# Two bf16 products of zeros per batch, into the unused columns of an attention kernel's PSUM tile

## The chip, the cores and the metric

The kernel runs on one core of a Trainium2 chip. The metric is the device time of one execution in microseconds. The kernel before takes 3329.91 us, the median of three runs (3328.71 to 3332.3).

## The reference, cut to what matters

Four layers of a graph network run one after the other on 6250 nodes with 128 features and 106,250 edges sorted by target (each node has a loop to itself); each layer ends in a residual and a layer norm. The change lies in the last, a graph attention with H = 3 heads:

```python
alpha = a_src[row2] + a_dst[col2] + a_edge
alpha = jnp.where(alpha >= 0, alpha, NEG_SLOPE * alpha)
m = jax.ops.segment_max(alpha, col2, num_segments=n)
ex = jnp.exp(alpha - m[col2])
denom = jax.ops.segment_sum(ex, col2, num_segments=n)
attn = ex / denom[col2]
msg = attn[:, :, None] * xp[row2]
agg = jax.ops.segment_sum(msg, col2, num_segments=n)
y = (agg.reshape(n, H * OUT) + gat_bias) @ lin_W + lin_b
```

Then comes the sum of `x` and `y`, a layer norm with weights, the outer residual and the last layer norm. The kernel sums the rows of `x` by attention weight first, and multiplies by the product of the two weight matrices (`mh`) afterwards, in `end`.

## The kernel before, in words

The function `by_windows` holds all four layers. The first three fill the first 2250 us of the profiled execution: sums over edges as bf16 products of one-hot matrices (L819), gathers by GpSimd (L774), and dense layers. They are not touched.

The attention works in NBT = 208 batches of BT = 4 tiles of 128 edges. The targets of a batch lie in a window of BW = 40 nodes, so H x BW = 120 columns hold the weights of a tile. A batch has S = 6 slices: the last tile of the batch before, its own four, and one with the loops of its nodes.

- `fetch(b)` (L1061) gathers the source rows of four tiles with four indirect DMAs from GpSimd's queue (L1065), into one of eight buffers `rows3`. It runs AHEAD = 5 batches ahead.
- `weigh(b)` loads the loop rows (SyncE, L1119), forms the logits `z` (L1121, `lrelu` L315), a mask (L1129, L1134), and `w`, the masked logits of 6 x 120 columns (L1136). Six TensorE transposes bring it to PSUM (`w_p`, L1141), and VectorE takes the maximum per head and node (`mx`, L1144).
- `power(b)` brings that maximum back to 128 partitions with a transpose into a slot of the PSUM tile `both` (L1148), subtracts it (VectorE, L1151), and ScalarE takes the exponential (L1153).
- `gather(b)` makes the weighted sums: six fp32 products accumulate in the PSUM tile `o`, 120 x 132 (L1162; each is two records in the trace). Columns 0 to 127 are features and 131 is the sum of weights. Then the reciprocal (VectorE, L1164), the scaling (ScalarE, L1166), a transpose into `both` (L1168), and the copy into `acc` (L1169).
- `end(blocks)` (products at L1102) finishes 500 nodes, after each sixteenth or so batch.

The source loop issues `power(b - 1)`, `gather(b - 2)`, `fetch(b + 5)`, `weigh(b)` and, where due, `end`. A scheduler then lays out the instructions of each engine anew; each engine works through its own list in order. So the order of L1141, L1148, L1162 and L1168 on TensorE is not that of the source, and changes from batch to batch. Every fourth batch the window bases are read into registers (L307).

Of the kernel before, what the change touches and what calls it, by code (L numbers as in the profile page):

```python
# [8 lines left out]
F32 = mybir.dt.float32  # L9
# [10 lines left out]
F = 128  # L20
# [5 lines left out]
H = 3  # L26
# [14 lines left out]
BT, NBT, BW = 4, 208, 40  # L41
# [5 lines left out]
BF16 = mybir.dt.bfloat16  # L47
# [8 lines left out]
def gnn_kernel(ctx: ExitStack, tc: tile.TileContext, a: dict, out: bass.AP):  # L56
# [135 lines left out]
    with tc.If(ordered) as cond:  # L192
        by_windows(tc, a, out, consts, ix)
# [9 lines left out]
def by_windows(ctx: ExitStack, tc: tile.TileContext, a: dict, out: bass.AP, consts, ix):  # L203


    nc = tc.nc
# [50 lines left out]
    def by_block(table, blocks):  # L257
        return table[blocks[0] * PB:(blocks[-1] + 1) * PB, :].rearrange("(b p) f -> p b f", p=PB)
# [5 lines left out]
    def row_over(x, nb):  # L264

        return x.rearrange("p (b f) -> p b f", b=1).to_broadcast([PB, nb, x.shape[1]])
# [33 lines left out]
    def bases(at, n, engine, last=N - 1):  # L300

        got = {}

        def of(g):
            if g % 4 == 0:
                m = min(4, n - g)
                _, v = nc.values_load_multi_w_load_instructions(  # L307
                    ix["base"][0:1, at + g:at + g + m], engines=[engine], min_val=0, max_val=last,
                    skip_runtime_bounds_check_because=WITHIN)
                got.update({g + i: y for i, y in enumerate(v)})  # L310
            return got[g]
        return of

    def lrelu(x):
        nc.vector.scalar_tensor_tensor(x, x, 0.2, x, op0=OP.mult, op1=OP.max)  # L315
# [120 lines left out]
    for c in range(GC):  # L436
        for k in range(RT):
            nc.tensor.matmul(counts[:, c:c + 1], lhsT=below[:, k, c * 128:(c + 1) * 128], rhs=oneb,
                             start=(k == 0), stop=(k == RT - 1))
# [270 lines left out]
    with tc.tile_pool(name="l0w", bufs=2) as work, \  # L710
# [5 lines left out]
        for blocks in CHUNKS:  # L716
# [18 lines left out]
            for j in range(nb):  # L735
                for m in range(4):
                    nc.tensor.matmul(yp[:PB, j, :], lhsT=ht[:, m, j * PB:(j + 1) * PB], rhs=w2[:, m, :],  # L737
                                     start=(m == 0), stop=(m == 3))
# [319 lines left out]
    S = BT + 2  # L1058
    rows = {}

    def fetch(b):  # L1061
        own = min(BT, 831 - b * BT)
        r = rows[b] = gp.tile([128, BT, XW], F32, name="rows3")
        for j in range(own):
            nc.gpsimd.indirect_dma_start(  # L1065
                out=r[:, j, :], out_offset=None, in_=x3,
                in_offset=bass.IndirectOffsetOnAxis(ap=ix["src"][:, BT * b + j:BT * b + j + 1], axis=0))
        if own < BT:
            nc.vector.memset(r[:, own:BT, :], 0.0)
# [11 lines left out]

    l3b = ctx.enter_context(tc.tile_pool(name="l3b", bufs=1))
    acc = l3b.tile([128, H, NW], F32, name="acc3")
    of_sp, of_dve = bases(NG, NBT, SP), bases(NG, NBT, DVE)
    with tc.tile_pool(name="lr", bufs=5) as lrp, \
            tc.tile_pool(name="zb", bufs=4) as zbp, tc.tile_pool(name="ob", bufs=2) as obp, \
            tc.tile_pool(name="wb", bufs=3) as wbp, tc.tile_pool(name="fin", bufs=1) as fin, \
            tc.tile_pool(name="fps", bufs=1, space=bass.MemoryType.PSUM) as fps, \
            tc.tile_pool(name="tps", bufs=2, space=bass.MemoryType.PSUM) as tps, \
            tc.tile_pool(name="ops", bufs=2, space=bass.MemoryType.PSUM) as ops, \  # L1090
            tc.tile_pool(name="mps", bufs=1, space=bass.MemoryType.PSUM) as mps:
        both = mps.tile([128, 4, H, BW], F32, name="both")
        loops_, zs, ws, ms = {}, {}, {}, {}

        def end(blocks):


            b0, nb = blocks[0], len(blocks)
            p = fps.tile([128, 4, F], F32, name="fp")
            for j, b in enumerate(blocks):  # L1100
                for h in range(H):
                    nc.tensor.matmul(p[:PB, j, :], lhsT=acc[:, h, b * PB:(b + 1) * PB], rhs=mh[:, h, :],  # L1102
                                     start=(h == 0), stop=(h == H - 1))
            x = xn[:PB, b0:b0 + nb, :]
            y, z, o = (fin.tile([128, 4, F], F32, name=n)[:PB, :nb, :] for n in ("yf", "zf", "of"))
            nc.vector.tensor_tensor(y, x, row_over(cb[:PB], nb), op=OP.add)
            nc.vector.tensor_add(y, y, p[:PB, :nb, :])
            layernorm(z, y)
            nc.vector.tensor_tensor(z, z, row_over(lng[:PB], nb), op=OP.mult)
            nc.vector.tensor_tensor(z, z, row_over(lnb[:PB], nb), op=OP.add)  # L1110
            nc.vector.tensor_add(z, z, x)
            layernorm(o, z)
            nc.sync.dma_start(by_block(out, blocks), o)

        def weigh(b):

            r = rows[b]
            loop = loops_[b] = lrp.tile([128, XW], F32, name="loop")
            nc.sync.dma_start(loop, x3[ds(of_sp(b), 128), :])  # L1119
            z = zs[b] = zbp.tile([128, S, H], F32, name="z")  # L1120
            nc.vector.tensor_add(z[:, 1:1 + BT, :], r[:, :, F:F + H], zed[:, BT * b:BT * (b + 1), :])  # L1121
            lrelu(z[:, 1:1 + BT, :].rearrange("p j h -> p (j h)"))
            nc.scalar.copy(z[:, S - 1, :], loop[:, F + H + 1:F + 2 * H + 1])
            if b:
                nc.scalar.copy(z[:, 0, :], zs.pop(b - 1)[:, BT, :])
            else:
                nc.vector.memset(z[:, 0, :], 0.0)
            oh = wbp.tile([128, S, 1, BW], F32, name="oh3")
            nc.vector.tensor_tensor(oh[:, :, 0, :],  # L1129
                                    iota[:, 0:BW].rearrange("p (j w) -> p j w", j=1).to_broadcast([128, S, BW]),  # L1130
                                    ix["relb"][:, b, :].rearrange("p (j w) -> p j w", w=1).to_broadcast([128, S, BW]),
                                    op=OP.is_equal)

            nc.vector.tensor_scalar(oh, oh, -1.0, -LOW, op0=OP.add, op1=OP.mult)  # L1134
            w = ws[b] = wbp.tile([128, S, H, BW], F32, name="w3")
            nc.vector.tensor_tensor(w, oh.to_broadcast([128, S, H, BW]),  # L1136
                                    z.rearrange("p j (h w) -> p j h w", w=1).to_broadcast([128, S, H, BW]),
                                    op=OP.add)
            tp = tps.tile([H * BW, 2, 512], F32, name="w_p")
            for j in range(S):  # L1140
                nc.tensor.transpose(tp[:, j // 3, j % 3 * 128:(j % 3 + 1) * 128],  # L1141
                                    w[:, j, :, :].rearrange("p h w -> p (h w)"), ident)
            mx = ms[b] = zbp.tile([H * BW, 1], F32, name="mx")
            nc.vector.tensor_reduce(mx, tp[:, :, 0:384], AX.XY, OP.max)  # L1144

        def power(b):
            mb = both[:, b % 2]
            nc.tensor.transpose(mb.rearrange("p h w -> p (h w)"), ms.pop(b).to_broadcast([H * BW, 128]),  # L1148
                                ident[:H * BW, :H * BW])
            wf = ws[b].rearrange("p j h w -> p j (h w)")  # L1150
            nc.vector.tensor_tensor(wf, wf, mb.rearrange("p (j h) w -> p j (h w)", j=1)  # L1151
                                    .to_broadcast([128, S, H * BW]), op=OP.subtract)
            nc.scalar.activation(wf, wf, AF.Exp)  # L1153

        def gather(b):
            wf = ws.pop(b).rearrange("p j h w -> p j (h w)")
            loop = loops_.pop(b)
            r0 = rows.pop(b - 1)[:, BT - 1, 0:F + H + 1] if b else loop[:, 0:F + H + 1]
            o = ops.tile([H * BW, F + H + 1], F32, name="o")
            for j in range(S):  # L1160
                rr = r0 if j == 0 else loop[:, 0:F + H + 1] if j == S - 1 else rows[b][:, j - 1, 0:F + H + 1]
                nc.tensor.matmul(o, lhsT=wf[:, j, :], rhs=rr, start=(j == 0), stop=(j == S - 1))  # L1162
            rd = zbp.tile([H * BW, 1], F32, name="rd")
            nc.vector.reciprocal(rd, o[:, F + H:F + H + 1])  # L1164
            on = obp.tile([H * BW, F], F32, name="on")
            nc.scalar.activation(on, o[:, 0:F], AF.Copy, scale=rd)  # L1166
            ot = both[:, 2 + b % 2]
            nc.tensor.transpose(ot.rearrange("p h w -> p (h w)"), on, ident[:H * BW, :H * BW])  # L1168
            nc.vector.tensor_copy(acc[:, :, ds(of_dve(b), BW)], ot)  # L1169


        for b in range(NBT + 2):
            if 1 <= b <= NBT:
                power(b - 1)
            if b >= 2:
                gather(b - 2)
            if b + AHEAD < NBT:
                fetch(b + AHEAD)
            if b < NBT:
                weigh(b)  # L1180
            for k, d in enumerate(DONE):
                if d == b - 2:
                    end(CHUNKS[k])
# [692 lines left out]
```

## Time and profile before

| | |
|---|---|
| median of 3 runs | 3329.91 us (3328.71 to 3332.3) |
| the profiled execution | 3577.21 us |
| its span, first to last instruction | 3575.3 us |
| mean granted TensorE clock over the span | 0.82 |
| before 2250 us / after it | 0.87 / 0.74 |
| TensorE busy, span | 2624.6 us (73%) |
| VectorE busy, span | 1837.7 us (51%) |
| GpSimd busy, span | 1671.1 us (47%) |
| ScalarE busy, span | 910.8 us (25%) |
| busy after 2250 us (1325.3 us): PE / DVE / POOL / ACT | 800.3 / 845.6 / 806.5 / 361.2 us |

Times are of one profiled execution, which is longer than the runs without a profile. PE is TensorE's products, PEld its weight loads, DVE VectorE, ACT ScalarE, POOL GpSimd, SP SyncE. A row of slices cuts the span in 40 parts and shows the busy tenths of each; PEclk is the granted share of TensorE's clock in tenths. "x <- y" in the list of waits reads: x's engine sat idle until y had ended. "issue", "remote" and "an unknown queue" are waits of which the trace does not show the end. The ends of TensorE's products are modelled.

### The profile page before, as it was taken

What the parts mean: (1) busy time and instruction counts of PE and PEld (TensorE: products, weight loads), DVE (VectorE), ACT (ScalarE), POOL (GpSimd) and SP (SyncE); (2) the same over time, 40 slices, a digit from 0 to 9 for tenths busy, and PEclk for the clock granted to TensorE, in tenths of its full rate; (3) what the DMA queues carried; (4) which work ended last, traced back from release to release, by engine and by line L of the source; (5) the groups of instructions that cost most, each with busy time, mean ns of one, the idle gap of its engine ahead of it and who ended that gap; (6) DMA issues with size and microseconds to landing.
All of it is one profiled execution on the core that took longest, in us unless ns stands there. A gap on an engine that the chain in (4) does not pass through costs nothing.

```text
span 3575.3 us, 43560 instructions
## 1 busy us (share of the span) xinstructions
PE 2624.6 (73%) x14544; PEld 1618.5 (45%) x14544; DVE 1837.7 (51%) x6113; ACT 910.8 (25%) x1657; POOL 1671.1 (47%) x1684
## 2 busy tenths in 40 slices
PE   2788879899995599999787893666565666666565
PEld 1334335544442344445343342555554555555554
DVE  4899994478214800000211122666565666666666
ACT  0587874300002400002100010222222222222222
POOL 3000002277607755430556424666666666666662
PEclk9677779999997599999898896777777777777777
DMA  5588871387751356563665553222222222222221
GB/s 155 167 278 279 274 248 48 105 245 228 220 164 51 82 181 205 182 183 96 184 179 153 169 166 90 52 58 58 54 61 58 56 57 58 55 60 59 57 58 33
DMA packets 333524, 461.85 MB, mean 129 GB/s; under 512 B 43998, under 2 KB 217854, under 8 KB 332933
## 3 DMA queue, kind: packets, MB, share of 16 engines
q1 hardware_dynamic: 250754, 278.98, 26.2%
q0 software_dynamic: 54912, 105.86, 12.4%
q10 hardware_dynamic: 27624, 74.14, 5.6%
q8 instruction: 117, 1.92, 0.2%
q14 instruction: 117, 0.96, 0.1%
HBM read 375.30 MB, written 83.36 MB: 128 GB/s over the span
## 4 chain that ended last, share of the span: by engine, by line
PE 52%; DVE 22%; issue 12%; DMA 4%; POOL 3%; another core or an unknown queue 3%; ACT 2%; DVEq 1%; SPq 0%; ACTq 0%; POOLq 0%
PE sums L819 25%; PE o L1162 10%; DVE okey L616 5%; DVE olow L614 4%; PE w_p L1141 4%; POOL nd L416 2%; DVE w L1151 2%; PE both L323 2%; DVE w L1136 1%; PE yp L995 1%; ACT w L1153 1%; PE yp L737 1%; PE fp L1102 1%; DVE mx L1144 1%
## 5 line engine op out<-in xcount | busy, mean ns | idle before, releaser
L1065 POOL DMA_INDIRECT rows<-x,srca x831 | 841.5, 1013 | 490.3 <-issue 213.4
L819 PE MATMUL sums<-piece,arena 125*128 125x500 bf16 x4500 | 1021.1, 383 | 51.1 <-issue 40.0
L819 PEld LDWEIGHTS <-arena 125*128 125x128 bf16 x4500 | 435.6, 98 | 591.4 <-issue 122.4
L774 POOL DMA_INDIRECT row<-table,srca x549 | 542.1, 987 | 335.7 <-issue 142.5
L1162 PE MATMUL o<-rows,w 128*120 128x132 f32 x2078 | 440.1, 364 | 245.1 <-issue 132.2
L1162 PEld LDWEIGHTS o<-rows,w 128*120 128x120 f32 x2078 | 378.1, 255 | 290.1 <-issue 159.7
L619 ACT CAST arena<-made 128x1000 bf16<-128x1000 f32 (+1 forms) x260 | 313.5, 1262 | 63.9 <-PE made L617 55.9
L1153 ACT ACTIVATE w<-w 128x720 f32<-128x720 f32 x208 | 167.0, 803 | 521.6 <-DVE w L1151 368.5
L617 PE MATMUL made<-okey,olow 128*128 128x250 bf16 x1000 | 248.4, 330 | 62.4 <-ACT arena L619 28.4
L616 DVE TENSOR_SCALAR okey<-iok,key 128x250 bf16<-128x250 bf16 x1000 | 289.6, 290 | 0.0
L1141 PE MATMUL w_p<-ident,w 128*120 128x128 f32 x1248 | 230.7, 328 | 65.1 <-DVE w L1136 39.1
L1144 DVE TENSOR_REDUCE mx<-w_p 120x1 f32<-120x768 f32 x208 | 198.0, 952 | 151.7 <-PE o L1162 82.6
L1151 DVE TENSOR_TENSOR w<-w,both 128x720 f32<-128x720 f32 x208 | 187.1, 900 | 162.0 <-remote 89.1
L614 DVE TENSOR_SCALAR olow<-iob,low 128x128 bf16<-128x128 bf16 x1000 | 254.7, 255 | 0.0
L1141 PEld LDWEIGHTS w_p<-ident,w 128*120 128x120 f32 x1248 | 187.2, 169 | 80.3 <-issue 49.6
L325 ACT COPY by_node<-both 128x128 f32<-128x128 f32 (+1 forms) x48 | 12.7, 265 | 756.6 <-PE both L323 479.8
L334 DVE TENSOR_TENSOR onehot<-iota,relg 128x384 f32<-128x384 f32 x118 | 64.2, 547 | 272.7 <-PE both L323 140.9
L617 PEld LDWEIGHTS <-olow 128*128 128x128 bf16 x1000 | 108.0, 113 | 184.9 <-DVE okey L616 89.6
L1136 DVE TENSOR_TENSOR w<-oh,z 128x720 f32<-128x720 f32 x208 | 186.7, 898 | 0.2 <-DVE acc L1169 0.2
L690 POOL MEMSET ea<- 128x128 f32 x1 | 0.5, 465 | 397.9 <-PE sums L323 397.9
L1168 PE MATMUL both<-ident,on 120*128 120x120 f32 x208 | 70.3, 338 | 108.2 <-DVE w L1151 95.2
L1148 PE MATMUL both<-ident,mx 120*128 120x120 f32 x208 | 73.0, 351 | 91.2 <-DVE acc L1169 69.6
(283 smaller groups left out, 3188.5 us busy)
## 6 DMA issues: line engine op xcount, KB each, us to landing
piece<-edges SPq DMA_DIRECT2D x300, 625.0 KB
edges<-arena ACTq DMA_DIRECT2D x100, 625.0 KB
ea<-in_edge_attr_dram SPq DMA_DIRECT2D x69, 768.0 KB
loop<-x SPq DMA_DIRECT2D x208, 68.0 KB
rows<-x,srca POOLq DMA_INDIRECT x831
row<-table,srca POOLq DMA_INDIRECT x549
eat<-in_edge_attr_dram POOLq DMA_DIRECT2D x28, 236.0 KB
table<-xn SPq DMA_DIRECT2D x24, 250.0 KB
```

The source lines that it names most:

```text
L614: nc.vector.tensor_scalar(o, iob, low[:, g:g + 1], None, op0=OP.is_equal)
L616: nc.vector.tensor_scalar(w, iok, key[:, g:g + 1], None, op0=OP.is_equal)
L617: nc.tensor.matmul(p[:, i, 0:NB5 * GD], lhsT=o, rhs=w, start=True, stop=True)
L619: nc.scalar.copy(to, p[:, 0:n, 0:NB5 * GD].rearrange("p i (h d) -> p i h d", d=GD))
L774: nc.gpsimd.indirect_dma_start(out=r[:, j, :], out_offset=None, in_=table, in_offset=bass.IndirectOffsetOnAxis(ap=ix["src"][:, t:t + 1], a ...
L819: nc.tensor.matmul(p, lhsT=xp[:PB, h, i, :], rhs=t[:PB, :, (h - h0) * SC:(h - h0 + 1) * SC], start=(h == 0 and i == 0), stop=(h == NB5 - 1 ...
L1065: nc.gpsimd.indirect_dma_start(out=r[:, j, :], out_offset=None, in_=x3, in_offset=bass.IndirectOffsetOnAxis(ap=ix["src"][:, BT * b + j:BT ...
L1136: nc.vector.tensor_tensor(w, oh.to_broadcast([128, S, H, BW]), z.rearrange("p j (h w) -> p j h w", w=1).to_broadcast([128, S, H, BW]), op= ...
L1141: nc.tensor.transpose(tp[:, j // 3, j % 3 * 128:(j % 3 + 1) * 128], w[:, j, :, :].rearrange("p h w -> p (h w)"), ident)
L1144: nc.vector.tensor_reduce(mx, tp[:, :, 0:384], AX.XY, OP.max)
L1151: nc.vector.tensor_tensor(wf, wf, mb.rearrange("p (j h) w -> p j (h w)", j=1) .to_broadcast([128, S, H * BW]), op=OP.subtract)
L1162: nc.tensor.matmul(o, lhsT=wf[:, j, :], rhs=rr, start=(j == 0), stop=(j == S - 1))
```

## The change

A tile `zeros` of 128 x 512 bf16 is filled with zeros once by GpSimd. The PSUM tile `o` grows from 132 to 512 columns[...]. In each batch a product of zeros (120 x 380, bf16) is written into its columns 132 to 511 before the six products of sums, and another after them. Nobody reads those columns.

```diff
+    zeros = l3b.tile([128, 512], BF16, name="zeros")
+    nc.gpsimd.memset(zeros, 0.0)
...
+        def idle(to):
+
+            nc.tensor.matmul(to, lhsT=zeros[:, 0:H * BW], rhs=zeros[:, 0:to.shape[1]], start=True, stop=True)
+
...
-            o = ops.tile([H * BW, F + H + 1], F32, name="o")
+            o = ops.tile([H * BW, 512], F32, name="o")
+            idle(o[:, F + H + 1:])
             for j in range(S):
                 rr = r0 if j == 0 else loop[:, 0:F + H + 1] if j == S - 1 else rows[b][:, j - 1, 0:F + H + 1]
-                nc.tensor.matmul(o, lhsT=wf[:, j, :], rhs=rr, start=(j == 0), stop=(j == S - 1))
+                nc.tensor.matmul(o[:, 0:F + H + 1], lhsT=wf[:, j, :], rhs=rr, start=(j == 0), stop=(j == S - 1))
+            idle(o[:, F + H + 1:])
```

The scheduler sees the new instructions, and its order of the others changes too, on TensorE, VectorE and ScalarE from the first batches of the attention on. SyncE's order stays, and GpSimd's but for the one memset.

## The prediction

> **What bounds the kernel now.** First the page: the time slices say where the change acts. It touches only the attention loop, so I looked for the first product into `o` (L1162), at 2251.8 us of a span of 3575.3 us. Everything before it is issued in the same order in both builds.
>
> ```profile
> PE   2788879899995599999787893666565666666565
> DVE  4899994478214800000211122666565666666666
> POOL 3000002277607755430556424666666666666662
> PEclk9677779999997599999898896777777777777777
> ```
>
> From slice 26 on no engine is full: PE, DVE and POOL are busy six tenths each, and PE was granted 0.7 of its clock, against 0.9 in the stage of L819. The loop has 208 batches in some 1308 us, 6.3 us each. Next came the chain of work that ended last, restricted to 2250 to 3560 us, and the waits there.
>
> ```profile
> by line: PE o L1162 26.7%; issue 20.5%; PE w_p L1141 10.3%; another core or an unknown queue 7.9%; DVE w L1151 4.2%; DVE w L1136 3.9%; ACT w L1153 3.4%; DVE mx L1144 3.0%; PE fp L1102 2.9%; PE both L1148 2.7%; PE both L1168 1.5%; DVEq L307
> ```
>
> (the waits: who, for what, us in total, times, longest)
>
> ```profile
> POOL rows L1065 <- PE o L1162: 176.2, 81, 11.4
> ...
> PE o L1162 <- ACT w L1153: 110.1, 80, 6.7
> ...
> DVE w L1151 <- remote: 89.1, 29, 6.4
> ```
>
> PE's products are 44% of this chain (26.7+10.3+2.9+2.7+1.5), so what PE's clock does counts. The gathers wait for PE (their row buffers are freed by L1162), not PE for them. PE in turn waits for the exponential. The stage is a ring of PE, DVE and ACT, and no single engine is the limit.
>
> Then the granted clock, in stretches cut on its own steps, 3.41 us long (columns: stretch, length, busy PE, PEld, DVE, ACT, POOL with counts, clock, DMA):
>
> ```profile
> 2614.42:2617.83 3.41, 1.71 (x9) 1.67 (x9) 3.02 (x8) 0.43 (x2) 2.80 (x3) 0.50 0.22 47
> 2617.83:2621.25 3.42, 3.31 (x16) 2.90 (x15) 2.36 (x5) 1.21 (x4) 2.53 (x3) 0.50 0.29 62
> 2621.25:2624.66 3.41, 2.46 (x21) 2.22 (x21) 3.23 (x8) 1.25 (x3) 2.77 (x3) 1.00 0.34 82
> 2624.66:2628.07 3.41, 1.04 (x10) 0.80 (x8) 1.05 (x2) 0.00 (x0) 2.50 (x4) 1.00 0.18 41
> 2628.07:2631.49 3.42, 2.39 (x11) 2.39 (x11) 0.22 (x2) 1.25 (x3) 1.51 (x2) 0.50 0.36 82
> ```
>
> The 0.7 is a mean of two values, 0.50 and 1.00. A stretch with PE busy 3.31 of 3.42 us is followed by a fast one; a fast stretch with 1.04 of 3.41 is followed by a slow one. I did this for all 360 stretches from 2331 us on. Of 77 changes to fast, 73 came after a busy share of 0.85 or more. Of 76 changes to slow, 68 came after a share under 0.45. The fast share is 48%. What it is worth shows in two rounds of the same order, slow then fast:
>
> ```profile
> 2618.45 1.23 PE L1162 MATMUL o<-rows,w 128*120 128x132 f32 x4
> 2619.68 1.53 PE L1162 MATMUL o<-rows,w 128*120 128x132 f32 x6
> 2623.22 0.71 PE L1162 MATMUL o<-rows,w 128*120 128x132 f32 x4 [0.95 <-ACT w L1153]
> 2623.88 0.84 PE L1162 MATMUL o<-rows,w 128*120 128x132 f32 x6
> ```
>
> Starts of neighbouring records are 0.22 us apart when slow, 0.11 when fast. With 12 records for `o`, 6 for `w_p` and one for each of the two into `both`, PE needs 20 x 0.22 = 4.4 us a batch slow, 2.2 us fast.
>
> **The change part by part.** *The products themselves.* The nearest row is the bf16 product of L819: 1021.1 us for 4500 products of 500 columns, 0.227 us each at clock 0.9 to 1. For 380 columns that is 0.173 us fast and, doubled, 0.345 us slow. Two in each of 208 batches: 72 us of PE time if always fast, 144 us if always slow. Their weight loads lie beside products, as L819's do. How much is on the path? The built order puts the first one ahead of `o`'s first matmul, which waits for the exponential (the 110.1 us above), mostly in a gap; the second comes right after the last `o`. Behind that second one are queued the six transposes L1141, for which the maximum L1144 waits. The reciprocal L1164 now also waits for it: in the built program its semaphore value counts the second product, and in 28 of 208 batches also a transpose L1148 that stands between. L1164 comes after the 0.9 us subtraction L1151 on DVE, which hides most of that. If all were on the path it would cost 208 x 2 x (0.67 x 0.173 + 0.33 x 0.345) = 96 us at the fast share I expect below; by PE's 44% of the chain 42 us; I take 30 us, a third, since one of the two stands before a wait. It can't gain by itself.
>
> *The clock.* Each product adds 0.05 (fast) to 0.10 (slow) to the busy share of a stretch. 27 of the 76 falls to slow came from shares of 0.35 to 0.45: I count those as saved, so falls go from 76 of 172 fast stretches (0.44) to 49 (0.28). Of 110 slow stretches that stayed slow 30 had shares of 0.70 to 0.85: those I count as raised, so rises go from 77 of 187 slow stretches (0.41) to 107 (0.57). Balance: 0.57/(0.57+0.28) = 0.67 fast, up 0.19. Over the PE timeline the 73 rounds of the commonest order lasted 6.09 us when over three quarters slow (23 rounds) and 5.03 us when over three quarters fast (27), 1.06 us less. 0.19 x 208 x 1.06 = 42 us gained. The PE time alone (2.2 x 0.19 x 208 x 44%) would give 38. Bounds: 0, and 0.19 x 208 x 2.2 = 87 us.
>
> Here the Trainium skill ("TensorE: Matmul & The Clock Gate", Part 1) speaks differently: the clock falls only after an idle window of about 3.4 us. By that two products a batch, which leave no stretch idle, would end every fall, and 0.52 x 208 x 1.06 = 115 us would come back. The trace refuses it: falls come from stretches busy up to 0.45. I go by the rows. The same page (Part 4) says that transposes do not count as PE activity in the same way, which would leave the shares lower; but a threshold over all products misplaces 12 of 358 stretches, one without transposes 49. They count here.
>
> *The order.* The scheduler lays the loop out anew. In 91 of the 207 rounds of before, a transpose L1148 stands inside or ahead of L1141's six in a cycle of three rounds; by the PE timeline these 91 took 573 us, 6.30 each, the commonest order 5.85. In the new build these cycles are gone (163 rounds are of the common kind). 91 x 0.45 = 41 us. But 29 of these 91 hold the 29 unexplained waits of L1151 (89.1 us); if those are not due to the order nothing is left. Bounds 0 and 41; I take 20.
>
> *The rest.* One memset on POOL, 0.5 us (the nearest is L690's, 0.465 us), queued among the first gathers, which are five batches ahead: nothing. Without that lead 0.5 us. SyncE's order is the same; POOL's gathers follow in the same order. The new tile fills a bank, with as many buffers as before: no new wait for `o` beyond its readers, which the transpose L1168 has waited for already.
>
> Sum: 30 - 42 - 20 = -32 us, from 3577.2 us (span 3575.3) to about 3545. The profiled execution is 247 us longer than the median of 3329.9; the stage's chain holds 28% of "issue" and unknown waits, some of which may exist only under the profiler. I carry the difference over as it is: 3298 us.
>
> **The rivals.** *Slower: the price without the clock.* In the stretches just after the last `o`, the second product delays L1141, the maximum, and so the next subtraction, in every batch; if the fast share does not rise, the two cost 2 x (0.48 x 0.173 + 0.52 x 0.345) = 0.53 us a batch, 109 us of PE time. A third of that is 36 us, with no gain: 3366 us. It decides from a rise of the fast share under 30/(208 x 1.06) = 0.14. For it: 41 of the 76 falls came from shares under 0.35 or so, and two products do not mend these. Against it: the thresholds are sharp, and zeros keep PE busy as any data does.
>
> *No change: POOL sets the pace.* While a gather does not wait it starts 1.25 us after the one before (0.94 busy, 0.30 "issue"), so 831 need 1039 us of the stage's 1308. If the 247 us that the profile adds lie in this stage, 1061 are left without it, and the gathers are nearly the bound: whatever PE gains is hidden, 3330 less a few us. Against it: POOL waited 176 us for PE.
>
> *The full gain.* Falls nearly end, as the skill's rule has it, and the order gives 20 as above: 30 - 115 - 20 = -105, 3225 us. For it speaks that each fall saved leaves PE faster and the ring shorter; against it the 41 falls from low shares.
>
> **How the numbers follow.** Mine (3265 to 3321, about 3298): 0.40. The full gain: 0.12. POOL's pace, within 0.2%: 0.15. Slower: 0.33. 0.2% (7 us) is about what a measurement of this kernel can tell from no change. Faster is 0.40+0.12 = 0.52. The range, 3240 to 3372, leaves out about 0.08 below (part of the full gain) and 0.12 above (products wholly on the path in slow stretches). Alone, my case has 3265 to 3321.
>
> **What would show it.** The mean clock after 2250 us: 0.74 before, (1+0.67)/2 = 0.84 by my count; under 0.80 the slower rival decides. The new products' starts 0.17 us ahead of what follows. L1141's and L1164's waits on PE: longer by under 0.15 us a batch. The unexplained waits of L1151: gone if they were the order's. POOL's waits for L1162: from 176 us towards 0 if POOL becomes the bound. I am wrong if the clock rises and the time doesn't, or if the fast share stays where it is.

## The result and the profile after

The kernel after takes 3321.15 us, the median of 8 runs (3315.76 to 3323.84), beside 3333.56 us for the kernel before on the same chip (8 runs, 3328.71 to 3342.4). The ratio is 0.9958, with an interval of 0.9947 to 0.9969. That makes it 14 us faster (12 us between the two medians, since the ratios here are not plain quotients of medians), where 32 had been forecast. The profiled execution of after took 3318.93 us, and its span is 3317.1 us.

The slices of the span of after:

```profile
PE   2788788979999549999988899366666666666666
DVE  4899996448722380000031112287767777777766
POOL 2100002058751776553056652467777777777774
PEclk6676778989999759999999899688888888888878
```

In the attention (slice 26 on) the granted clock is 8 where the page of before had 7, as forecast. But VectorE and GpSimd are busier too, 7 where they had 6, although they do the same work: the stage itself is shorter, 1142 us from the first product into `o` to the end (2174.7 to 3317.1), against 1324 (2251.8 to 3575.3). Those 181 us are far more than the runs differ. So the two pages can't be laid side by side as "before and after"; something else lies between them.

The chain of work that ended last, and the waits, from 2250 to 3317 us:

```profile
by line: DMA rows<-x,srca 17.6%; PE o L1169 16.7%; issue 10.9%; DVE w L1157 10.1%; POOL rows L1065 7.8%; ACT w L1159 6.9%; DVE w L1142 4.9%; DVE mx L1150 3.2%; PE w_p L1147 2.7%; PE fp L1104 2.6%; DVE acc L1177 1.5%; PE both L1154 1.5%; DVE
```

```profile
PE o L1169 <- ACT w L1159: 239.4, 167, 13.0
DVE z L1127 <- DMA rows<-x,srca: 196.1, 82, 4.5
...
POOL rows L1065 <- PE o L1169: 46.0, 63, 3.3
```

A row stands here that the chain of before did not have: the arrival of gathered rows, 17.6%, and with the gathers themselves (L1065) a quarter of the chain. The first logits of a batch wait 196.1 us for rows. In the page of before they never waited for them, and the gathers waited 176.2 us for PE. The waits of L1151 on "remote", 89.1 us, are gone.

The new products in the groups of the page of after, and one pair in the timeline (columns there: start, length, instruction):

```profile
L1119 PE MATMUL o<-zeros 128*120 128x380 bf16 x416 | 133.1, 352 | 0.7 <-POOL zeros L1085 0.7
```

```profile
2178.86 0.33 PE L1119 MATMUL o<-zeros 128*120 128x380 bf16 x1
2179.03 0.82 PE L1147 MATMUL w_p<-ident,w 128*120 128x128 f32 x6
```

A record lasts 0.33 us, but what follows starts 0.17 us after it. Over all pairs without a gap the median is 0.16 us at the full clock and 0.32 us at half: the forecast of 0.173 and 0.345 us a product was right.

### The profile page after: what moved, and what is told of

Read it like the earlier page. It is cut to its first block, busy times and chain, and to the rows that moved or that the text cites. A ratio compares the mean times of both kernels' runs of the same rounds, so it can differ in the third digit from the quotient of the medians.

```text
span 3317.1 us, 44206 instructions
## 1 busy us (share of the span) xinstructions
PE 2536.9 (76%) x14960; PEld 1547.6 (47%) x14960; DVE 1831.8 (55%) x6113; ACT 902.3 (27%) x1657; POOL 1675.9 (51%) x1685
## 4 chain that ended last, share of the span: by engine, by line
PE 35%; DVE 13%; DMA 10%; POOL 7%; issue 7%; ACT 3%; DVEq 1%; POOLq 0%; SPq 0%; ACTq 0%
PE sums L819 21%; DMA rows<-x,srca 6%; PE o L1169 6%; DVE w L1157 4%; POOL rows L1065 3%; ACT w L1159 2%; POOL nd L416 2%; DVE w L1142 2%; DMA row<-table,srca 2%; POOL row L774 2%; PE yp L995 1%; DVE mx L1150 1%; PE w_p L1147 1%; PE both L323 1%; PE fp L1104 1%
## 5 line engine op out<-in xcount | busy, mean ns | idle before, releaser
L819 PE MATMUL sums<-piece,arena 125*128 125x500 bf16 x4500 | 1000.7, 379 | 10.0 <-DMA piece<-edges 10.0
L1065 POOL DMA_INDIRECT rows<-x,srca x831 | 849.5, 1022 | 309.1 <-issue 174.9
L1169 PE MATMUL o<-rows,w 128*120 128x132 f32 x2078 | 359.5, 316 | 255.2 <-ACT w L1159 255.1
L1169 PEld LDWEIGHTS o<-rows,w 128*120 128x120 f32 x2078 | 306.1, 211 | 308.9 <-ACT w L1159 308.6
L616 DVE TENSOR_SCALAR okey<-iok,key 128x250 bf16<-128x250 bf16 x1000 | 281.0, 281 | 0.0
L614 DVE TENSOR_SCALAR olow<-iob,low 128x128 bf16<-128x128 bf16 x1000 | 246.3, 246 | 0.0
L1147 PE MATMUL w_p<-ident,w 128*120 128x128 f32 x1248 | 196.3, 297 | 26.9 <-DVE w L1142 26.5
L1150 DVE TENSOR_REDUCE mx<-w_p 120x1 f32<-120x768 f32 x208 | 197.5, 950 | 23.2 <-PE w_p L1147 21.7
L1147 PEld LDWEIGHTS w_p<-ident,w 128*120 128x120 f32 x1248 | 160.5, 150 | 55.8 <-issue 27.8
L1127 DVE TENSOR_TENSOR z<-rows,zed 128x12 f32<-128x12 f32 x208 | 34.5, 166 | 206.2 <-DMA rows<-x,srca 206.2
L1119 PE MATMUL o<-zeros 128*120 128x380 bf16 x416 | 133.1, 352 | 0.7 <-POOL zeros L1085 0.7
```

Of the source, the lines that this page charges most:

```text
L614: nc.vector.tensor_scalar(o, iob, low[:, g:g + 1], None, op0=OP.is_equal)
L616: nc.vector.tensor_scalar(w, iok, key[:, g:g + 1], None, op0=OP.is_equal)
L819: nc.tensor.matmul(p, lhsT=xp[:PB, h, i, :], rhs=t[:PB, :, (h - h0) * SC:(h - h0 + 1) * SC], start=(h == 0 and i == 0), stop=(h == NB5 - 1 ...
L1065: nc.gpsimd.indirect_dma_start(out=r[:, j, :], out_offset=None, in_=x3, in_offset=bass.IndirectOffsetOnAxis(ap=ix["src"][:, BT * b + j:BT ...
L1169: nc.tensor.matmul(o[:, 0:F + H + 1], lhsT=wf[:, j, :], rhs=rr, start=(j == 0), stop=(j == S - 1))
```

## The experiments

They ran on four chips, here called A, B, C and D. Every ratio is to the kernel before on the same chip. The theories that the expectations weigh, in short: *clock and order*, the forecast's own (the clock, or the new order of instructions, brings the gain); *price* (the products cost what the clock brings); *gathers* (GpSimd's gathers set the pace, so little of what PE gains reaches the end).

### Chip A: the same kernel, 250 us longer

On this chip the clock was to be parted from the order. First the kernel before once more, unchanged:

> The kernel before, unchanged, for a second profile. Its profiled execution was 247 us longer than its median, and 77 us of that lay ahead of the attention, where nothing changed. Theory A (the profile of before was disturbed; without that the attention is paced by the gathers): the new profile has a span near 3330 us, an attention of some 1155 us instead of 1323, a wait of the logits for the gathered rows of 150 us or more, and a fast share of the clock near 0.5 to 0.6. Theory B (the late ends of TensorE's products belong to this order of instructions under the profiler): span near 3575 us again, with the 29 unknown waits of the subtraction. Time: ratio 1.000 by both.

Measured: 3584.08 us, ratio 1.0007 (0.9985 to 1.0028); on this chip the kernel before takes 3581.23 us (59 runs). So the 3577.21 us of the first profile need no profiler to explain them: all 22 runs here took 3562 to 3603 us, and on chip C (below) a profiled execution is as long as the median. They are what this kernel takes on such a chip, while the median of 3329.91 us came from another. (The chip of the first profile is not known; its time and its waits are those of chip A.) The waits of this run after 2250 us show what the chip does:

```profile
POOL rows L1065 <- PE o L1162: 153.1, 66, 13.0
...
PE o L1162 <- issue: 112.5, 74, 3.6
...
DVE w L1151 <- remote: 63.0, 23, 4.4
```

The rows "issue" for PE and "remote" for VectorE are its visible trace; the list of the same kernel on chip C has neither. They go with late signals. In the attention of this run there are 205 places where the signal (a semaphore event) of a product comes 0.15 to 8 us after the last product that the trace has as ended, 304 us in sum; in the first profile there are 183, 285 us in sum; in the profile of after none. The sums are rough, since the traces of this kind lack one in eight of the signals (7288 of 8315 are there).

The ends of products are modelled, so products that really last longer would look alike. They are not the whole of it: between 2649.42 and 2649.67 us seven signals come 0.04 us apart, while neighbouring products start 0.11 us apart at the closest. What holds the signals up is not known.

*Both products, eight columns wide.* The tile, the waits and the count of instructions are those of the change, PE's added work is nearly gone. The scheduler's order goes back to the cycles of three rounds of the kernel before.

```diff
-            nc.tensor.matmul(to, lhsT=zeros[:, 0:H * BW], rhs=zeros[:, 0:to.shape[1]], start=True, stop=True)
+            nc.tensor.matmul(to[:, 0:8], lhsT=zeros[:, 0:H * BW], rhs=zeros[:, 0:8], start=True, stop=True)
```

> Both products stay, with 8 columns instead of 380: the tile, the waits and the number of instructions are those of the change, TensorE's added time is next to nothing, and the scheduler's order goes back to three-round cycles as before (26 and 21 rounds with the maximum's transpose inside the six, against 29 and 23 before, and none in the change). If the gain comes from the order or from the clock: no gain, ratio 0.998 to 1.003. If it comes from the tile or the waits: 0.996.

Measured: 3583.67 us, 1.0016 (0.9994 to 1.0037).

*Only the second product, 128 columns wide.* This gives the regular order (nearly all rounds alike) with a sixth of the added columns.

```diff
-            idle(o[:, F + H + 1:])
             for j in range(S):
...
-            nc.tensor.matmul(to, lhsT=zeros[:, 0:H * BW], rhs=zeros[:, 0:to.shape[1]], start=True, stop=True)
+            nc.tensor.matmul(to[:, 0:128], lhsT=zeros[:, 0:H * BW], rhs=zeros[:, 0:128], start=True, stop=True)
```

> Only the second product, with 128 columns: a third of its width and none of the first, so the clock gets about a sixth of the change's activity, but the order is the regular one of the change (154 common rounds, no three-round cycles). If the order makes the gain: ratio 0.996 (-12 us). If the clock does: 0.999 (-2 us).

Measured: 3574.11 us, 0.9998 (0.9979 to 1.0017); the medians alone would make it 0.998.

*Only the second product, whole (380 columns).*

```diff
-            idle(o[:, F + H + 1:])
             for j in range(S):
```

> Only the second product, whole, in nearly the same order as the run with 128 columns (129 and 24 common rounds against 132 and 22). If the order makes the gain: 0.996, as with 128 columns. If the clock does: about half to two thirds of the change's gain, 0.998 (-7 us), and a fast share of the clock between that of before and 0.69.

Measured: 3576.65 us, 0.999 (0.9967 to 1.0013). The clock after 2250 us was 0.76, against 0.74 in the run of before. On this chip none of the three is distinguished from the kernel before, and the 20 us that I had given to the order do not show. The unexplained waits of the subtraction on "remote" do not end with the order either: 63.0 us (before) and 70.1 us (narrow products) in the old one, 54.2 us (128 columns) and 38.4 us (380) in the regular one. The changed kernel itself was not run on this chip. So it stays open whether the forecast, made from a profile of this kind, would have held here.

### Chip B: a quarter of the gathers taken away

If the gathers set the pace, then with fewer of them the time falls by up to 207 x 1.25 = 259 us, and only then can what PE gains be seen. In each of the 207 full batches the fourth gather was replaced by a plain load from SyncE of 128 fixed rows. The fourth tile is thus computed with other rows; bytes and instructions of the rest stay.

```diff
-        for j in range(own):
+        if own == BT:
+            nc.sync.dma_start(r[:, BT - 1, :], x3[0:128, :])
+        for j in range(min(own, BT - 1)):
```

The changed kernel unchanged, for the reference on this chip:

> The changed kernel itself, timed again beside the kernel before. Where the kernel before takes some 3333 us, the first result should come back: 0.996. Where it takes some 3580 us, TensorE's ends come up to several us late in every kernel seen so far; if the products of zeros help by the clock, the gain there is larger than 12 us, since TensorE is then the slow part of the ring (0.98 to 0.99); if they only add work to a TensorE that is late anyway, 1.00 or above.

Measured: 3325.16 us against 3328.93, 0.9989 (0.9979 to 1.0). The gain is smaller here, 4 us, at the edge of the interval.

The kernel before, with three gathers:

> The kernel before, with the fourth of the four gathers of a batch replaced by a plain load of 128 fixed rows on SyncE's queue, so the sums take other rows than the reference's. GpSimd's time per batch falls from 5.0 to 3.75 us; every other instruction and its order stay. If the gathers pace the attention, the kernel gets faster by 40 to 150 us (ratio 0.955 to 0.988), down to what the ring of TensorE, VectorE and ScalarE needs. If the ring paces it: within 10 us of before (0.997 to 1.003).

Measured: 3127.14 us, 0.9392 (0.9368 to 0.9416).

The changed kernel, with three gathers:

> The changed kernel with the same replacement of the fourth gather. If the gathers hide the change's gain, it shows here: this kernel is faster than the one of before with three gathers by clearly more than 12 us (20 to 80 us). If the products cost as much as the clock gives back, the two kernels with three gathers are within 12 us of each other, or this one is the slower.

Measured: 3128.07 us, 0.9397 (0.9375 to 0.9418).

A quarter of the gathers was worth 202 us of the 259: they largely set the pace of the attention on this chip. But behind them the change gains nothing either: from the first product into `o` to the end the two profiles take 948.8 and 949.3 us. By the expectation that speaks for the other theory, that the products cost as much as the clock gives back. What bounds the kernel then, the busy times of the last 955 us, the chain and the waits say (columns: stretch, length, busy PE, PEld, DVE, ACT, POOL with counts, clock, DMA share, GB/s). First the kernel before with three gathers, its chain, and waits in it:

```profile
2170.00:3125.00 955.00, 658.84 (x4472) 585.76 (x4471) 844.80 (x2254) 360.66 (x903) 616.23 (x600) 0.88 0.33 77
```

```profile
by line: PE o L1164 25.4%; DVE w L1153 13.4%; ACT w L1155 9.9%; issue 9.6%; DVE w L1138 5.5%; PE w_p L1143 5.5%; DVE mx L1146 4.3%; DMA rows<-x,srca 3.7%; DVE oh L1131 2.8%; DVE oh L1136 2.7%; POOL rows L1067 2.1%; DVEq L307 1.9%; PE both L
```

```profile
POOL rows L1067 <- PE o L1164: 124.4, 68, 28.2
...
DVE z L1123 <- DMA rows<-x,srca: 29.9, 15, 3.3
DVE rd L1166 <- PE o L1164: 27.3, 33, 1.1
```

Then the changed kernel with three gathers:

```profile
2170.00:3125.00 955.00, 699.34 (x4874) 606.95 (x4874) 838.87 (x2253) 357.38 (x902) 615.86 (x600) 0.91 0.33 78
```

VectorE is the busiest engine, 844.80 of 955 us or 88%, and its wait for rows has shrunk to 29.9 us. But no engine is full, and the products of `o` are the largest single row of the chain, 25.4%: the stage is a ring of PE, VectorE and ScalarE again. That VectorE hides what PE gains is possible and not shown. That the products' price takes up what the clock gives back (0.88 to 0.91) fits these rows as well.

*Only the second product, 128 columns, on this chip.*

> The second product alone with 128 columns, in the regular order, once more, beside the changed kernel on the same chip. If the order makes the change's gain: the same ratio as the changed kernel. If the clock does: at most a third of its gain.

Measured: 3326.73 us, 0.999 (0.9978 to 1.0002): the same ratio as that of the whole change on this chip, and no more certain.

### Chip C: before and after in profiles of one chip, and six products

The kernel before and the changed kernel, both unchanged, for two profiles of one chip:

> The kernel before, unchanged, for a profile on a chip on which it takes some 3330 us (if this call gets one). If the gathers pace the attention there: span near 3330 us, the logits wait for gathered rows for 150 us or more, TensorE's products end when the trace says, the clock after 2250 us near 0.80, and GpSimd waits for TensorE for under 60 us. If the ring paces it: GpSimd waits for TensorE for 150 us or more. Ratio 1.000.

> The changed kernel a third time, to settle the size: the two results so far are 0.9958 (0.9947 to 0.9969) and 0.9989 (0.9979 to 1.0000). If the gathers hide its gain, 0.997 to 1.000; if the first result is the true size, 0.996. On a chip where TensorE's ends come late (before near 3580 us): between 0.985 and 1.005, not known.

Measured: 3329.65 us, 0.9997 (0.9988 to 1.0006), and 3321.69 us, 0.9968 (0.9955 to 0.9981). The stretch from 2170 us on, the chain and the waits there, of before:

```profile
2170.00:3327.00 1157.00, 695.74 (x4469) 624.19 (x4469) 852.02 (x2261) 362.26 (x904) 812.37 (x801) 0.81 0.27 64
```

```profile
by line: PE o L1162 19.8%; issue 14.0%; POOL rows L1065 13.3%; DMA rows<-x,srca 10.7%; DVE w L1151 8.6%; ACT w L1153 6.6%; PE w_p L1141 4.6%; DVE w L1136 3.1%; PE fp L1102 2.8%; DVE mx L1144 2.5%; PE both L1148 1.4%; DVE oh L1129 1.3%; DVEq
```

```profile
DVE z L1121 <- DMA rows<-x,srca: 199.6, 75, 4.5
...
POOL rows L1065 <- PE o L1162: 66.9, 68, 12.7
```

and of the changed kernel:

```profile
2170.00:3327.00 1157.00, 745.25 (x4885) 640.35 (x4885) 849.26 (x2261) 355.98 (x904) 819.18 (x802) 0.86 0.27 64
```

```profile
DVE z L1127 <- DMA rows<-x,srca: 216.5, 95, 4.9
...
POOL rows L1065 <- PE o L1169: 48.0, 66, 3.3
```

This is the pair to read for the clock and the waits. It is no pair to read the gain from: the profiled execution of the changed kernel is the longest of its nine, and the two spans are 3327.7 and 3326.9 us.

The wait for rows, 199.6 us, stands in the kernel before as well, and so do the gathers with the arrival of their rows, 24.0% of its chain (13.3 and 10.7). So the change did not bring them. The clock rises from 0.81 to 0.86; by the count of stretches the fast share goes from 0.63 to 0.72. PE does 50 us more work in the same time.

Little of this reaches the gathers. Their waits for the last readers of their buffers fall from 66.9 to 48.0 us, but other waits take the place: 799 gathers start after the first product into `o`, and beyond 1.25 us for each they lose 115 us in the kernel before and 116 in the changed one. VectorE waits 17 us longer for rows.

The ring itself is quicker here than in the first profile. I cut PE's timeline into rounds at the first product into `o` of each batch. The 72 rounds of the commonest order in the kernel before (73 in the forecast) last 3.56 us on this chip, against 5.87 in the first profile, and 68 of them have over three quarters of their time at the full clock, against 27. Other rounds are longer, and the mean is 5.46 us; a batch's four gathers take 5.0 us.

*Six products.* Three at each of the two places, in a regular order, though not quite that of the change.

```diff
             idle(o[:, F + H + 1:])
+            idle(o[:, F + H + 1:])
+            idle(o[:, F + H + 1:])
             for j in range(S):
...
             idle(o[:, F + H + 1:])
+            idle(o[:, F + H + 1:])
+            idle(o[:, F + H + 1:])
```

> Six products of zeros per batch, three at each place, in the regular order. By the prediction's third on the path, the four more cost 4 x 0.19 x 208 / 3 = 53 us, so some 1.012 to 1.016. If the gathers pace the attention, TensorE has slack for them: 0.998 to 1.003, with a granted clock above 0.92 after 2250 us.

Measured: 3328.58 us, 0.9994 (0.9983 to 1.0006).

```profile
2170.00:3327.00 1157.00, 841.33 (x5725) 726.08 (x5723) 841.46 (x2252) 359.33 (x903) 837.23 (x804) 0.90 0.27 64
```

```profile
DVE z L1127 <- DMA rows<-x,srca: 247.4, 113, 4.5
```

The time is what the theory of the gathers had expected. The clock rises again, to 0.90 (above 0.92 had been expected), and PE is as busy as VectorE and GpSimd. The time does not fall with it: the gain of two products is gone, and VectorE waits 247.4 us for rows.

The same with three gathers (the fourth tile again has the fixed rows):

> Six products per batch with three gathers and one plain load (other rows than the reference's are summed). With the gathers out of the way, the change with two products took as long as the kernel before, 3128 and 3127 us. If VectorE, 0.89 busy there, is the next bound and hides TensorE: 3125 to 3140 us (0.939 to 0.943). If products are paid once the gathers no longer pace: 3165 us or more (0.951).

Measured: 3114.4 us, 0.9358 (0.9342 to 0.9374), at a clock of 0.95 in the attention. That is 13 us under the kernel before with three gathers on chip B (0.9392, 0.9368 to 0.9416). It is below both expected ranges, so it speaks against a price that is paid and against VectorE as a floor at 3125 us. A gain of the clock beyond the gathers is possible. But this comparison of two chips does not show it: the ratio of one and the same kernel moves as far from chip to chip, as the next section shows.

### Chip D: the small differences again

> The changed kernel a fourth time. Where the kernel before takes some 3330 us: 0.996 to 0.999, as the three results so far. Where it takes some 3580 us, as in the profile that the prediction was made from: the prediction's sum gives 0.991 (-32 us); if the late ends of TensorE's products set the pace there, as the second product alone suggests (0.999), 0.997 to 1.002.

> Six products per batch once more. Where before takes some 3330 us: 0.999, as measured. Where it takes some 3580 us: if the clock is what counts there, faster than with two products; if TensorE's late ends count, slower (1.005 to 1.02).

> Both products with 8 columns, in an order like that of before, on a second chip if it gets one. Where before takes some 3330 us: if the order makes the small gain, 1.000; if the tile, the waits or the mere number of instructions do, 0.997.

Measured, against 3333.24 us (48 runs): the changed kernel 3326.38 us, 0.9979 (0.9969 to 0.9988); six products 3342.33 us, 1.003 (1.0021 to 1.004); both products eight columns wide 3333.38 us, 1.000 (0.9989 to 1.001). For six products 0.999 had been expected: their two intervals, on C and on D, do not meet, and neither do those of the change in the first result and on B. The intervals leave out what differs from chip to chip, some 0.003.

So in three of four comparisons the interval of the change leaves out 1 (0.9958 in the first, 0.9968 on C, 0.9979 on D); on B, 0.9989, it ends there. The gain is 4 to 14 us by the ratios, 4 to 12 by the medians. The tile of 512 columns, the added waits and 416 more instructions change nothing beyond 0.1%, as the narrow products show here, in the old order. Four products more than the change has cost 0.0026 (C) and 0.0051 (D) of 3330 us: 9 and 17 us.

## Why the prediction was right and wrong

The direction was right, and the clock rose by the mechanism that was forecast. The size was wrong, and that the sign came out right is partly luck: with the clock and the order as they turned out, the sum would have been 30 - 20 - 0 = +10 us.

**The step that failed** is the two gains in the sum, -42 us for the clock and -20 us for the order. Both were sized on the first profile, and then "I carry the difference over as it is" took them to runs of another regime. On chips B, C and D the signals of PE are not late, and there:

- the fast share starts at 0.63 (chip C) and not at 0.48, and rises by 0.09 and not by 0.19, worth 20 us at my own 1.06 us a batch;
- the unexplained waits of L1151, 89.1 us in the first profile, do not exist in either order;
- "no single engine is the limit" no longer holds. The stage takes 1146 us instead of 1324 (before, chip C: 2181.3 to 3327.7), and 799 gathers at 1.25 us each fill 999 of them. With 207 gathers fewer the kernel is 202 us shorter.

I had the gathers among the rivals, gave them 0.15, and spoke against them with 176 us of waits that on chip C are 66.9. (Their 1039 us count all 831 gathers; 32 start ahead of the stage.) They are not the whole account. If they alone hid the gain, it would have come out with three gathers, and it did not: 3127.14 and 3128.07 us. What hides it there stays open.

**Where the 247 us lay.** The forecast held that they might "exist only under the profiler". They exist without it, on some chips. Before against before, 70 of them lie ahead of the attention (first product into `o` at 2251.8 us, on chip C at 2181.3 us) and 177 in it.

**The clock**, -42 us: the mechanism held, the size did not. The thresholds hold on chip C too: 50 of 53 rises came after a busy share of 0.85 or more, 44 of 52 falls after one under 0.45. The rise was smaller for two reasons. One is the start: 68 of the 72 commonest rounds there ran fast already. The other is a slip in my count. It saved falls from shares of 0.35 up, as if each stretch held two fast products; but a batch of 6.3 us holds two, so a stretch of 3.41 us holds 1.1, which adds 0.055 fast and 0.11 slow. With these widths 15 falls are saved and not 27, 20 stretches are raised and not 30, and the fast share comes to 0.59 and not 0.67: up 0.11, and 24 us.

The forecast's own sign, a mean clock of 0.84 after 2250 us, is what the profile of after has (0.84 for 2250 to 3317). That it fits is luck: the kernel before has 0.81 there on chip C, not 0.74.

The Trainium skill's idle window ("TensorE: Matmul & The Clock Gate", Part 1), the basis of the full gain, is refused once more. With six products a batch on chip C the clock still falls 38 times, and before 26 of these falls PE had not stood idle for 3.4 us at a stretch (products and weight loads, over the 6.8 us ahead of the fall).

**The price**, +30 us for two products: the 0.173 us of each was right; a third of it on the path looks too much for these chips, since the sum above would make the change slower. Four further products, 60 us by that rule, cost 9 and 17 us net of the little clock that they bring. No run parts the price from the gain of the clock.

**The order**, -20 us: on chips B, C and D the 29 unexplained waits of L1151 do not exist, in either order. They belong to a chip like A, with its late signals, and even there the regular order keeps 54.2 and 38.4 us of them. Whether the order or the clock brings the remaining 4 to 14 us is not settled. The old order with narrow products gives 1.000; the regular order with one product of 128 columns gives 0.999 (0.9978 to 1.0002), which agrees both with no effect and with the 0.9989 of the whole change on the same chip. A kernel with the regular order and next to no PE work was not run: with eight columns the scheduler goes back to the old order.

**The slower rival** decided "from a rise of the fast share under 0.14". The rise was 0.09, and the kernel is still faster, so either the price was smaller than that rival's 36 us or the clock was worth more than its rise here makes it. The maximum and the reciprocal did not come to wait longer: in the profile of after VectorE's reciprocal waits 24.0 us for the second product, 21 times, against 40.2 us for the last `o` in before on chip C, and the maximum 21.7 us for its transposes against 20.9.

## What to carry to other kernels

Before a sum is made against a profiled execution, compare its time with the median: where they are 7% apart, the profile shows another regime, and the engine that sets the pace in it may not be the one of the timed runs. Then ask which engine is the pace without the disturbance (here: gathers times their own interval, against the stage less what is unexplained), and give that case the larger chance. A higher TensorE clock then has little to win: here most rounds already ran fast, the gathers waited for the products of `o` for 67 us of 1146, and the change brought 4 to 14. And where added work is to lift a busy share over a threshold, count how much of it falls into one stretch.

## What the runs showed of the hardware

- One kernel, two lengths: 3581 us on chip A, 3329 to 3333 us on the other three. On A signals of products come up to 8 us after the last recorded end, some 300 us in sum over the attention; in the profiles of the others none is over 0.15 us late.
- The granted clock follows the busy share of stretches of 3.41 us. In the first profile 73 of 77 rises came after shares of 0.85 up and 68 of 76 falls after shares under 0.45, on chip C 50 of 53 and 44 of 52. Added work of zeros raises the mean clock in steps: 0.81, 0.86, 0.90 for none, two and six products a batch on chip C.
- Gathers that are queued back to back start every 1.25 us, 0.94 busy and 0.30 of "issue": 207 of 831 less took 202 us off an attention of 1146.
